# A two-layer graph-attention network: adjacency masks turned by the DMA engines instead of by TensorE

## The chip, the cores and the metric

The kernel runs on one core of one Trainium2 chip. The metric is the device time of one execution in microseconds; the kernel before took 3589.72 us (median of three runs, 3589.04 to 3592.5). PE is the matrix engine, PEld its weight loads, DVE the vector engine, ACT the scalar engine, POOL GpSimd, and SP the engine whose queue issues most DMA transfers.

## The reference, cut to what matters

N = 4096 nodes with 256 features. `adj` is a 4096 x 4096 matrix of zeros and ones in int32, the same for all attention layers. Three attention layers use it: one in network layer 0, two in network layer 1.

```python
x = x + _L0_gnn_ref(_layernorm(x), adj, ...)      # attention 1
x = x + _L0_ffn_ref(_layernorm(x), ...)           # 30 steps of tanh, silu, layernorm, 256x256 matmul
x = x + _L1_gnn_ref(_layernorm(x), adj, ...)      # attention 2 and 3
x = x + _L1_ffn_ref(_layernorm(x), ...)           # 6 experts, top 2
# one attention layer, 4 heads of 64 columns:
h = einsum('nf,hfd->hnd', x, W)
e = leaky_relu(f1[:, :, None] + f2[:, None, :], 0.2)
e = where(adj > 0, e, -9e15)
out = elu(einsum('hnm,hmd->hnd', softmax(e, axis=-1), h))
```

## The kernel before

**An attention layer.** The exponential of a leaky ReLU is one of two products, each with one factor for the row n and one for the column m. Which one holds depends on whether f1[n] + f2[m] is positive. So the kernel never builds e: for each pair it needs a 0/1 mask "edge and positive" and a 0/1 mask "edge and not positive", multiplies each with values already scaled by their column's factor (`vals`, in two fp16 parts), and combines the two sums at the end with the row's factor `r`.

**Tiling.** Columns m lie on the partitions in 32 blocks of 128, taken in pairs q = 0 to 15. Rows n are taken in chunks. A chunk's mask of the edges is held in SBUF as four tiles `m` of 8 blocks x chunk rows in bf16, columns on partitions, rows along the free dimension: that is `adj` turned. The main loop (line 522) runs over chunk, head and q. In one step ACT makes `st`, the step function of f1 + f2, two instructions (L464); DVE makes `m1` from `st` and `m` (L533) and `m2 = m - m1` (L538); PE multiplies each 128 x 128 block of m1 and m2, as weights, with `vals` and adds into PSUM (L565). For 6 of the 16 q the mask is kept negative (0 and -1, `turned(q)`, the sign is in `vals`): then m1 comes from a `logical_and`, m2 is not needed, and PE uses m itself. At the end of a head ACT and DVE take the sums out of PSUM (`lo` L474, `u` L475), DVE and ACT finish the rows (L482 to L495) and SP stores them.

**Where the masks come from.** In the first layer `adj` must be turned. `load_rows` (L203) fetches 256 columns of a chunk's rows with a casting DMA from POOL's queue, int32 to bf16. `turn` (L212) turns each 128 x 128 block on PE into PSUM (`tp_m`, L217). `to_mask` (L222) compares on DVE and writes the mask to SBUF. It is stored turned in DRAM, `edges[block, partition, row]` (L74). The first chunk's masks are made in the preparation of the layer (`first_masks`, L229, called at L423) and are used straight from SBUF. Those of chunk c + 1 are made inside the main loop on chunk c: `make` (L500) is a generator that advances one piece per step (L540), turning, comparing and storing block by block (L514). `load_mask` (L195) fetches four tiles of a chunk with plain copies; it is issued in the last head of the chunk before, each time one of the four buffers has been used for the last time (L573). The second and third layers only load. The first layer has chunks of 4, 7, 7, 7 and 7 row tiles (L607), the others four chunks of 8 (L766).

**Preparation.** Before each main loop, eight groups of 512 rows are normalised, turned and multiplied with the weights (L268 to L394). In the first layer, the masks of the first chunk are made in between.

**Order.** SP issues its transfers in program order, each waiting for its own data; so a store of masks, a mask load and a load of `f1b` (L193) follow each other there. Casting loads are issued by POOL.

Of the kernel before, what the change touches and what calls it, by code (L numbers as in the profile page):

```python
# [11 lines left out]
F32 = mybir.dt.float32  # L12
BF16 = mybir.dt.bfloat16
# [14 lines left out]
G = 4  # L28
# [16 lines left out]
def gnn_ffn_kernel(ctx: ExitStack, tc: tile.TileContext, a: dict, out: bass.AP):  # L45
    nc = tc.nc
    x, adj = a["x"], a["adj"]
    N = x.shape[0]
    NT = N // P
# [8 lines left out]

    ident = const.tile([P, P], F32, name="ident")
    make_identity(nc, ident)  # L60
    ident16 = const.tile([P, P], BF16, name="ident16")
    nc.gpsimd.tensor_copy(ident16, ident)
    mone = const.tile([P, 1], F32, name="mone")
    nc.gpsimd.memset(mone, -1.0)
    ones = const.tile([2 * H, P], F32, name="ones")
# [5 lines left out]

    edges = dram.tile([NT, P, N], BF16, name="edges")  # L74
    fd = dram.tile([2 * H, N], F32, name="fd")

    x1d = dram.tile([N, C], F32, name="x1d")
# [4 lines left out]
    def rows_of(t, g):  # L82
        return t[g * GR : (g + 1) * GR, :].rearrange("(r p) c -> p r c", p=P)
# [3 lines left out]
    def rows_in():  # L87
        return stream.tile([P, G * C], F32, name="rows")
# [33 lines left out]


    def turned(q):
        return q % 8 in (1, 4, 6)


    sign = const.tile([P, NT], F32, name="sign")
# [42 lines left out]
    def attention(tag, src, norm, w, others, chunks, first, finish, following):  # L171
# [6 lines left out]
        with ExitStack() as scope:  # L178
# [6 lines left out]
            fpool = scope.enter_context(tc.tile_pool(name=f"{tag}_f", bufs=2))  # L185

            end = None if first else scope.enter_context(tc.tile_pool(name=f"{tag}_end", bufs=1))
            masks, arow, f1b = {}, {}, {}

            def load_f1(c, h):  # L190
                n0, w = starts[c] * P, chunks[c] * P
# [3 lines left out]
            def load_mask(c, g):  # L195

                n0, w = starts[c] * P, chunks[c] * P
                m = masks[c, g] = mask.tile([P, 8, CM * P], BF16, name="m")
                nc.sync.dma_start(
                    m[:, :, :w], edges[g * 8 : (g + 1) * 8, :, n0 : n0 + w].rearrange("j p n -> p j n")  # L200
                )

            def load_rows(c, j):  # L203
                nt = chunks[c]
                arow[c, j] = rows_in().bitcast(BF16).rearrange("p (t n) -> p t n", n=2 * P)

                nc.gpsimd.dma_start(  # L207
                    arow[c, j][:, :nt, :],
                    adj[starts[c] * P : (starts[c] + nt) * P, j * P : (j + 2) * P].rearrange("(t p) n -> p t n", p=P),
                )  # L210

            def turn(pool, c, j):  # L212

                nt = chunks[c]
                tp = pool.tile([P, 8 * P], BF16, name="tp_m")
                for t in range(nt):
                    nc.tensor.transpose(  # L217
                        tp[:, t * P : (t + 1) * P], arow[c, j - j % 2][:, t, (j % 2) * P : (j % 2 + 1) * P], ident16
                    )
                return tp  # L220

            def to_mask(dst, tp, c, j):  # L222
                w = chunks[c] * P
                if turned(j // 2):
                    nc.vector.tensor_scalar(dst[:, :w], tp[:, :w], 0.0, -1.0, op0=OP.is_le, op1=OP.add)
                else:
                    nc.vector.tensor_scalar(dst[:, :w], tp[:, :w], 0.0, None, op0=OP.is_gt)

            def first_masks(pool, j):  # L229

                g = j // 8
                if j % 8 == 0:
                    masks[0, g] = mask.tile([P, 8, CM * P], BF16, name="m")
                for jj in (j, j + 1):
                    to_mask(masks[0, g][:, jj % 8, :], turn(pool, 0, jj), 0, jj)
                if j % 8 == 6:
                    w = chunks[0] * P
                    nc.sync.dma_start(
                        edges[g * 8 : (g + 1) * 8, :, :w].rearrange("j p n -> p j n"), masks[0, g][:, :, :w]
                    )  # L240

            with ExitStack() as ps:
                prep = ps.enter_context(tc.tile_pool(name=f"{tag}_prep", bufs=1))
# [4 lines left out]
                ps_m = ps.enter_context(tc.tile_pool(name=f"{tag}_ppm", bufs=1, space=PSUM))  # L248
# [9 lines left out]
                def load(g):  # L258
                    if g in ahead:
                        rows[g] = ahead.pop(g)  # L260
                    elif first:
                        rows[g] = work.tile([P, G, C], F32, name="t", bufs=3)
                        nc.sync.dma_start(rows[g], rows_of(src, g))
                    else:
                        load_ahead(src, g)
                        rows[g] = ahead.pop(g)
# [126 lines left out]
                            op1=OP.add,  # L393
                        )  # L394

                if first:
                    for j in range(0, 6, 2):
                        load_rows(0, j)
                load(0)
                load(1)  # L400
                if not first:
                    load_mask(0, 0)
                made_masks = 0
                late = [functools.partial(make, prep, small_ps, get(prep)) for get, make in others]
                if late:
                    late.pop(0)()
                for g in range(NG + 2):
                    if g + 2 < NG:
                        load(g + 2)
                    if 2 <= g < NG:  # L410
                        columns(g)
                    if 1 <= g <= NG:
                        now = products(g - 1)
                    if 2 <= g:
                        lower(g - 2)
                    if g < 2:
                        columns(g)
                    if 1 <= g <= NG:
                        upper(g - 1, *now)
                    if first:  # L420
                        for _ in range(2 if g in (1, 2, 3, 4, 5, 6) else 1):
                            if made_masks < NT:
                                first_masks(ps_m, made_masks)  # L423
                                if made_masks + 6 < NT:
                                    load_rows(0, made_masks + 6)
                                made_masks += 2
# [4 lines left out]
                if first:  # L431
                    assert made_masks == NT
# [15 lines left out]

            if first:
                end = scope.enter_context(tc.tile_pool(name=f"{tag}_end", bufs=1))  # L450
                made = scope.enter_context(tc.tile_pool(name=f"{tag}_made", bufs=2))
            work = scope.enter_context(tc.tile_pool(name=f"{tag}_work", bufs=2))
            ps_o = scope.enter_context(tc.tile_pool(name=f"{tag}_pso", bufs=1, space=PSUM))
            ps_m = scope.enter_context(tc.tile_pool(name=f"{tag}_psm", bufs=1, space=PSUM)) if first else None
# [44 lines left out]

            def make(c):  # L500

                n0, w = starts[c] * P, chunks[c] * P
                load_rows(c, 0)
                load_rows(c, 2)
                for j in range(NT):
                    if j % 2 == 0:
                        st = made.tile([P, 2, CM * P], BF16, name="ms")
                        if j + 4 < NT:
                            load_rows(c, j + 4)
                    tp = turn(ps_m, c, j)  # L510
                    yield
                    to_mask(st[:, j % 2, :], tp, c, j)
                    if j % 2 == 1:
                        nc.sync.dma_start(  # L514
                            edges[j - 1 : j + 1, :, n0 : n0 + w].rearrange("j p n -> p j n"), st[:, :, :w]
                        )
                    if j < NT - 4:
                        yield

            step_of(*units[0])  # L520
            closing, making = None, None
# [81 lines left out]
    for n in range(2):  # L603
        av = a[f"L1_gnn_a{n + 1}"]
        for got, to in zip(weights(f"g{n + 1}", a[f"L1_gnn_W{n + 1}"], av[:, :D], av[:, D:], not n), (gw, makers)):
            to.append(got)
    attention("g0", x, True, w0, [make, *makers], [4, 7, 7, 7, 7], True, to_rows(x1d, x), [x1d])  # L607

# [583 lines left out]
```

## Time and profile before

| part of the trace | time |
|---|---|
| preparation of attention 1, up to the first product with a mask (L565) | 126.4 us |
| main loop of attention 1 (20 heads) | 126.4 us to about 812 us |
| feed-forward scan | to about 1895 us |
| attention 2, main loop | about 1982 us to 2579 us |
| attention 3, main loop | about 2642 us to 3242 us |
| experts | to 3587.7 us |

| engine | busy | share of the span |
|---|---|---|
| PE | 3264.7 us | 91% |
| DVE | 3002.9 us | 84% |
| ACT | 2615.2 us | 73% |
| POOL | 1100.6 us | 31% |

The page lists groups of instructions as "line, engine, operation, output<-inputs, shapes, count | busy time, mean time of one | idle time of the engine before them, and who ended it". A table by stretches gives, for each stretch of time, its length and then the busy time of each engine with the number of its instructions, the granted PE clock as a share of full speed, the share of the DMA engines' time that was busy, and GB/s. A DMA view names each queue with its packets, its MB, and the share of the 16 DMA engines' time that its packets took; q1 is the hardware queue behind SP, q0 the software queue behind POOL.

### The profile page before, as it was taken

To read this page: it belongs to the slowest core of one execution; us is meant where nothing else is said; L and a number is where in the kernel's file an instruction comes from. 1 tells how busy PE (TensorE), PEld (TensorE's weight loads), DVE (VectorE), ACT (ScalarE), POOL (GpSimd) and SP (SyncE) were. 2 spreads that over 40 slices of the span, in tenths; PEclk is the share of its full clock that TensorE was granted. 3 is DMA by queue.
4 is the path that set the end of the run, shared out by engine and by line. 5 is a ranking of instruction groups with operands and counts; after the bars stand their busy time and mean duration, and the time that the engine had idled before them with its cause. 6 is when DMAs were issued, how large, how long until landed. Compare 5 with 4: busy or idle time off the path is not lost. (4 is left out here: it accounts for less than half of the span.)

```text
span 3587.7 us, 81089 instructions
## 1 busy us (share of the span) xinstructions
PE 3264.7 (91%) x33523; PEld 2981.2 (83%) x33523; DVE 3002.9 (84%) x6039; ACT 2615.2 (73%) x2902; POOL 1100.6 (31%) x899
## 2 busy tenths in 40 slices
PE   6889999996999999999998899999979999996895
PEld 5779889885888888888886889888878888884784
DVE  6899999997877777877786899999889999997445
ACT  2688888886766666666663999999789999993221
POOL 3211101005877777777761000000000000001662
PEclk8899999998999999999998999999999999997897
DMA  6897887501000000000015031321212231314224
GB/s 136 145 232 141 192 196 135 168 22 55 1 1 1 1 1 1 1 1 1 1 31 194 17 119 33 125 75 66 85 66 78 89 123 44 119 25 135 83 95 182
DMA packets 280202, 288.48 MB, mean 80 GB/s; under 512 B 97149, under 2 KB 230426, under 8 KB 279834
## 3 DMA queue, kind: packets, MB, share of 16 engines
q1 hardware_dynamic: 198770, 224.18, 19.2%
q0 software_dynamic: 73920, 52.97, 9.7%
q10 hardware_dynamic: 7144, 6.16, 0.6%
q8 instruction: 264, 4.33, 0.5%
q14 instruction: 104, 0.85, 0.1%
HBM read 248.01 MB, written 68.81 MB: 88 GB/s over the span
## 5 line engine op out<-in xcount | busy, mean ns | idle before, releaser
L565 PE MATMUL acc<-vals,m 128*128 128x130 f16 (+1 forms) x24576 | 1726.6, 232 | 128.2 <-DVE u L475 89.0
L565 PEld LDWEIGHTS <-m 128*128 128x128 bf16 x24576 | 1625.2, 98 | 215.6 <-issue 95.5
L464 ACT ACTIVATE st<-f1b,f2b 128x1024 bf16<-128x1024 f32 (+2 forms) x1664 | 1660.2, 1071 | 152.6 <-DVE m L533 144.8
L533 DVE TENSOR_TENSOR m<-st,m 128x2048 bf16<-128x2048 bf16 (+2 forms) x832 | 938.1, 1137 | 37.0 <-PE acc L565 28.4
L708 PE MATMUL po<-wT,zT 128*128 128x256 f32 x3840 | 875.1, 381 | 10.3 <-ACT zT L734 10.1
L708 PEld LDWEIGHTS po<-wT,zT 128*128 128x128 f32 x3840 | 715.8, 192 | 99.8 <-ACT zT L734 12.4
L694 POOL TENSOR_TENSOR th<-th,y 128x1024 f32<-128x1024 f32 x240 | 567.8, 2367 | 196.2 <-ACT th L693 195.4
L538 DVE TENSOR_TENSOR m<-m,m 128x2048 bf16<-128x2048 bf16 (+2 forms) x520 | 592.8, 1140 | 25.1 <-PE tp_m L217 0.5
L105 POOL TENSOR_TENSOR ln_rstd<-ln_rstd,mhalf 128x4 f32<-128x4 f32 x272 | 281.7, 1036 | 904.1 <-DVE ln_rstd L104 877.3
L100 DVE BATCH_NORM_STATS2 ln_st<-z 128x6 f32<-128x256 f32 x960 | 337.9, 413 | 191.3 <-ACT z L699 191.3
L734 ACT COPY zT<-tp 128x1024 f32<-128x1024 f32 x240 | 242.8, 1012 | 323.7 <-PE tp L113 323.7
L718 DVE SCALAR_TENSOR_TENSOR y<-po,ln_rstd,bias 128x256 f32<-128x256 f32 x928 | 378.6, 469 | 5.2 <-PE po L708 4.4
L699 ACT ACTIVATE z<-th 128x1024 f32<-128x1024 f32 x240 | 254.5, 1060 | 18.5 <-POOL th L694 18.2
L113 PE MATMUL tp<-ident,z 128*128 128x128 f32 x1920 | 251.2, 274 | 12.3 <-ACT z L699 12.3
L113 PEld LDWEIGHTS tp<-ident,z 128*128 128x128 f32 x1920 | 225.9, 142 | 38.9 <-ACT z L699 15.3
L693 ACT ACTIVATE th<-y 128x1024 f32<-128x1024 f32 x240 | 251.2, 1047 | 4.8 <-DVE y L718 4.7
L207 POOL DMA_DIRECT2D rows<-in_adj_dram x80 | 72.9, 912 | 490.6 <-PE tp_m L217 490.3
L447 POOL MEMSET hs<- 128x4 f32 x3 | 0.3, 101 | 630.5 <-DVE u L488 609.1
L305 PE MATMUL ph<-g_w,xT 128*128 128x264 f32 x384 | 112.6, 454 | 30.9 <-DVE v L375 27.7
L305 PEld LDWEIGHTS ph<-g_w,xT 128*128 128x128 f32 x384 | 84.5, 227 | 50.8 <-issue 16.6
L1076 ACT COPY w<-ew 128x512 f32 x37 | 22.7, 617 | 132.8 <-PE ph L1083 103.5
L475 DVE TENSOR_TENSOR u<-acc,lo 128x520 f32<-128x520 f32 (+1 forms) x104 | 66.6, 654 | 49.0 <-ACT lo L474 48.8
(209 smaller groups left out, 2141.6 us busy)
## 6 DMA issues: line engine op xcount, KB each, us to landing
m<-edges SPq DMA_DIRECT2D x32, 2048.0 KB
rows<-in_adj_dram POOLq DMA_DIRECT2D x64, 448.0 KB, 8.0
edges<-ms SPq DMA_DIRECT2D x64, 448.0 KB
m<-edges SPq DMA_DIRECT2D x16, 1792.0 KB
f1b<-fd SPq DMA_DIRECT2D x32, 512.0 KB
rows<-x1d SPq DMA_DIRECT2D x16, 512.0 KB
y<-yd SPq DMA_DIRECT2D x16, 512.0 KB
f1b<-fd SPq DMA_DIRECT2D x16, 448.0 KB
```

The source lines that it names most:

```text
L100: nc.vector.bn_stats(st[:, r, :], src[:, r, :])
L105: nc.gpsimd.tensor_tensor(rstd, rstd, mhalf, OP.pow)
L113: nc.tensor.transpose(ps[:, k, r * P : (r + 1) * P], src[:, r, k * P : (k + 1) * P], ident)
L464: nc.scalar.activation(st[:, s, :w], f1b[c, h][:, :w], AF.Relu, bias=f2b[:, 2 * q + s, h : h + 1], scale=BIG)
L533: nc.vector.tensor_tensor(m1[:, :, :w], st[:, :, :w], m, OP.logical_and if turned(q) else OP.min)
L538: nc.vector.tensor_tensor(m2[:, :, :w], m, m1[:, :, :w], OP.subtract)
L565: nc.tensor.matmul(acc[:, i, cols], lhs[:, s, rows], v[:, cols], start=(j == 0 and n_ == 0), stop=(j == NT - 1 and n_ == 1), skip_group_ch ...
L693: nc.scalar.activation(th[at], y[:, g * G : (g + 1) * G, :], AF.Tanh, scale=0.01)
L694: nc.gpsimd.tensor_tensor(th[at], th[at], y[:, g * G : (g + 1) * G, :], OP.add)
L699: nc.scalar.activation(z, th.pop(at - 1), AF.Silu, scale=0.01)
L708: nc.tensor.matmul(po[:, r, :], src[:, k, r * P : (r + 1) * P], wT[:, k, :], start=(k == 0), stop=(k == KC - 1),)
L718: nc.vector.scalar_tensor_tensor(y[:, g * G + r, :], po[:, r, :], rstd[:, r : r + 1], last if end else bias, op0=OP.mult, op1=OP.add,)
```

## The change

The masks are no longer turned before they are kept. They are kept in DRAM row by row, as `adj` itself lies (`edges` is N x N), and each load of a mask tile is a transposing DMA. PE's turning and its PSUM tiles go away, and with them the comparison of a PSUM tile; DVE compares in place in SBUF, on the rows as they were loaded. A load of rows takes 2048 columns of one row tile (half its width) instead of 256 columns of a whole chunk. `to_masks` compares in three instructions: the q that are not turned in one or two patterns, the turned ones in another; so that a pattern with a fixed step can pick them, `turned(q)` becomes `q % 3 == 0`, again 6 of 16. The first chunk's four row tiles are loaded whole into the buffers that later hold the masks, compared, stored and loaded back turned; they too go through DRAM now. With the PSUM tiles gone, the first layer's chunks can be of 8 row tiles: 4, 4, 8, 8, 8. The maker of the next chunk's masks handles a half row tile in every third step. The rows of `x` in the first layer now come through the shared `rows` buffers.

```diff
-    edges = dram.tile([NT, P, N], BF16, name="edges")
+    edges = dram.tile([N, N], BF16, name="edges")
...
     def turned(q):
-        return q % 8 in (1, 4, 6)
+        return q % 3 == 0
...
                 m = masks[c, g] = mask.tile([P, 8, CM * P], BF16, name="m")
+                nc.sync.dma_start_transpose(m[:, :, :w], edges[n0 : n0 + w, g * 8 * P : (g + 1) * 8 * P])
+
+            def load_edges(dst, t, q):
+                nq = dst.shape[1]
+                nc.gpsimd.dma_start(
+                    dst, adj[t * P : (t + 1) * P, q * 2 * P : (q + nq) * 2 * P].rearrange("p (q n) -> p q n", n=2 * P)
+                )
+
+            def to_masks(rows, t, q):
+                nq = rows.shape[1]
+                a = -q % 3
+                b = a + (nq - a) // 3 * 3
+                plain = [rows[:, a:b].rearrange("p (i r) n -> p i r n", r=3)[:, :, 1:]]
+                plain += [x for x in (rows[:, :a], rows[:, b + 1 :]) if x.shape[1]]
+                for x in plain:
+                    nc.vector.tensor_scalar(x, x, 0.0, None, op0=OP.is_gt)
+                x = rows[:, a::3]
+                nc.vector.tensor_scalar(x, x, 0.0, -1.0, op0=OP.is_le, op1=OP.add)
                 nc.sync.dma_start(
-                    m[:, :, :w], edges[g * 8 : (g + 1) * 8, :, n0 : n0 + w].rearrange("j p n -> p j n")
+                    edges[t * P : (t + 1) * P, q * 2 * P : (q + nq) * 2 * P].rearrange("p (q n) -> p q n", n=2 * P), rows
                 )
-            def load_rows(c, j):
-            def turn(pool, c, j):
-            def to_mask(dst, tp, c, j):
-            def first_masks(pool, j):
...
+                if first:
+                    staged = []
+                    for t in range(chunks[0]):
+                        if t % 2 == 0:
+                            m = mask.tile([P, 8, CM * P], BF16, name="m")
+                            m = m.rearrange("p j n -> p (j n)")[:, : 2 * N].rearrange("p (t n) -> p t n", t=2)
+                        staged.append(m[:, t % 2].rearrange("p (q n) -> p q n", n=2 * P))
+                        load_edges(staged[t], t, 0)
...
+                        if 2 <= g < 2 + chunks[0]:
+                            to_masks(staged[g - 2], g - 2, 0)
+                        if g == 2 + chunks[0]:
+                            for i in range(4):
+                                load_mask(0, i)
...
             def make(c):
-                n0, w = starts[c] * P, chunks[c] * P
-                load_rows(c, 0)
-                load_rows(c, 2)
-                for j in range(NT):
...
+                halves = [(starts[c] + t, q) for t in range(chunks[c]) for q in (0, NJ // 2)]
+                got = {}
+                for i in range(-2, len(halves)):
+                    if i + 2 < len(halves):
+                        t = rows_in().bitcast(BF16).rearrange("p (q n) -> p q n", n=2 * P)
+                        got[i + 2] = t
+                        load_edges(t, *halves[i + 2])
+                    if i >= 0:
+                        for _ in range(3):
+                            yield
+                        to_masks(got.pop(i), *halves[i])
...
-    attention("g0", x, True, w0, [make, *makers], [4, 7, 7, 7, 7], True, to_rows(x1d, x), [x1d])
+    attention("g0", x, True, w0, [make, *makers], [4, 4, 8, 8, 8], True, to_rows(x1d, x), [x1d])
```

More of the change, by code (lines that the diff above doesn't have):

```diff
@@ L60, in gnn_ffn_kernel @@
     make_identity(nc, ident)
-    ident16 = const.tile([P, P], BF16, name="ident16")
-    nc.gpsimd.tensor_copy(ident16, ident)
     mone = const.tile([P, 1], F32, name="mone")
@@ L187, in attention @@
             end = None if first else scope.enter_context(tc.tile_pool(name=f"{tag}_end", bufs=1))
-            masks, arow, f1b = {}, {}, {}
+            masks, f1b = {}, {}
             def load_f1(c, h):
@@ L199, in load_mask @@
                 nc.sync.dma_start(
-                    m[:, :, :w], edges[g * 8 : (g + 1) * 8, :, n0 : n0 + w].rearrange("j p n -> p j n")
+                    edges[t * P : (t + 1) * P, q * 2 * P : (q + nq) * 2 * P].rearrange("p (q n) -> p q n", n=2 * P), rows
                 )
-            def load_rows(c, j):
[L204 to L210, printed above, removed]
@@ L212, in turn @@
-            def turn(pool, c, j):
[L214 to L220, printed above, removed]
-            def to_mask(dst, tp, c, j):
[L223 to L227, printed above, removed]
@@ L229, in first_masks @@
-            def first_masks(pool, j):
[L231 to L240, printed above, removed]
@@ L247, in attention @@
                 ps_h = ps.enter_context(tc.tile_pool(name=f"{tag}_pph", bufs=1, space=PSUM))
-                ps_m = ps.enter_context(tc.tile_pool(name=f"{tag}_ppm", bufs=1, space=PSUM))
                 xs = prep.tile([P, KC, NG], F32, name="xs")
@@ L260, in load @@
                         rows[g] = ahead.pop(g)
-                    elif first:
-                        rows[g] = work.tile([P, G, C], F32, name="t", bufs=3)
-                        nc.sync.dma_start(rows[g], rows_of(src, g))
                     else:
@@ L394, in lower @@
                         )
-                if first:
-                    for j in range(0, 6, 2):
-                        load_rows(0, j)
                 load(0)
                 load(1)
-                if not first:
+                if first:
[6 more added lines that the diff above has]
+                        load_edges(staged[t], t, 0)
+                else:
                     load_mask(0, 0)
-                made_masks = 0
                 late = [functools.partial(make, prep, small_ps, get(prep)) for get, make in others]
@@ L420, in attention @@
                     if first:
[L421 to L426, printed above, removed]
+                        if 2 <= g < 2 + chunks[0]:
[3 more added lines that the diff above has]
+                                load_mask(0, i)
                     elif g in (2, 4, 6):
@@ L430, in attention @@
                         late.pop(0)()
-                if first:
-                    assert made_masks == NT
                 nc.vector.tensor_tensor(r, fs[:, :, :H], mb.to_broadcast([P, NT, H]), OP.add)
@@ L450, in attention @@
                 end = scope.enter_context(tc.tile_pool(name=f"{tag}_end", bufs=1))
-                made = scope.enter_context(tc.tile_pool(name=f"{tag}_made", bufs=2))
             work = scope.enter_context(tc.tile_pool(name=f"{tag}_work", bufs=2))
             ps_o = scope.enter_context(tc.tile_pool(name=f"{tag}_pso", bufs=1, space=PSUM))
-            ps_m = scope.enter_context(tc.tile_pool(name=f"{tag}_psm", bufs=1, space=PSUM)) if first else None
             units = [(c, h, q) for c in range(len(chunks)) for h in range(H) for q in range(NJ)]
@@ L500, in make @@
             def make(c):
-                n0, w = starts[c] * P, chunks[c] * P
-                load_rows(c, 0)
-                load_rows(c, 2)
-                for j in range(NT):
[L506 to L518, printed above, removed]
+                halves = [(starts[c] + t, q) for t in range(chunks[c]) for q in (0, NJ // 2)]
[9 more added lines that the diff above has]
+                        to_masks(got.pop(i), *halves[i])
             step_of(*units[0])
```

## The prediction, made before the result

> **What bounds the kernel now.** I read the page's 40 slices first, to see which stage the change can reach. A slice is 89.7 us. Slices 1 to 9 are the first attention layer, 10 to 21 the feed-forward scan, 22 to 36 the other two attention layers, the rest the experts.
>
> ```profile
> PE   6889999996999999999998899999979999996895
> DVE  6899999997877777877786899999889999997445
> ACT  2688888886766666666663999999789999993221
> DMA  6897887501000000000015031321212231314224
> ```
>
> In all three attention layers PE, DVE and ACT are full together. What sets the first layer apart is DMA: 50 to 100% busy there, a tenth to a third in the other two. The edit acts on the first layer, and on the mask loads of all three.
>
> Second, busy time in stretches of one head each. The timeline of the SP queue gives their lengths: the loads of `old` and `f1b` come 24.0 to 24.2 us apart in the 4-tile chunk, 37.35 in 7-tile chunks that also make masks, 34.7 in the last 7-tile chunk, which makes none, and 37.26 to 37.5 in the 8-tile chunks of the later layers.
>
> ```profile
> core 0: us, PE busy (x) PEld busy (x) DVE busy (x) ACT busy (x) POOL busy (x), PEclk, DMA share, GB/s
> 300.00:337.35 37.35, 35.17 (x508) 33.75 (x506) 35.44 (x44) 31.96 (x35) 3.72 (x4) 0.95 0.67 125
> 686.00:720.70 34.70, 31.70 (x445) 30.19 (x443) 31.66 (x36) 31.73 (x36) 0.00 (x0) 0.95 0.11 28
> 2200.00:2237.30 37.30, 35.10 (x517) 33.37 (x515) 35.14 (x36) 35.36 (x36) 0.00 (x0) 1.00 0.08 26
> 160.00:184.00 24.00, 21.32 (x312) 19.60 (x311) 22.86 (x44) 20.97 (x35) 3.72 (x4) 1.00 1.03 177
> ```
>
> Read down the DVE and PE columns: mask making adds 3.8 us of DVE and 3.5 us of PE to a 7-tile head, yet the head grows by only 2.65. Third, the chain of waits inside one 8-tile head, where no masks are made:
>
> ```profile
> 2195.92 10.50 ACT st L464 x10
> 2206.41 0.50 ACT lo L474
> ...
> 2206.93 0.71 DVE u L475
> ...
> 2207.69 17.63 PE acc L565 x256
> ...
> 2225.67 1.23 DVE m L533
> ```
>
> The head is a ring of three nearly equal engines. At the head's end it narrows to lo, u, then the next matmul; there DVE waits 1.25 us for ACT and PE 1.8 us for DVE. Slack per engine is about 2 us, so work beyond that on one engine lengthens the head.
>
> **What the Trainium skill says.** "VectorE: DVE Perf Modes", section "The perf-mode tier table": a `tensor_scalar` on bf16 runs 4 elements a cycle from SBUF, at most 2 when an operand is in PSUM. The trace shows the PSUM half (896 columns in 618 ns, below) and no bf16 `tensor_scalar` in SBUF. "DMA: Bandwidth & Descriptors", section "Latency and other measured facts": a DMA transpose was measured at 261 GB/s with a non-contiguous middle dimension, 350 to 400 contiguous. The trace has no DMA transpose.
>
> **The change, part by part.** Removed from the first layer:
>
> ```profile
> L217 PE MATMUL tp_m<-ident,rows 128*128 128x128 bf16 x1024 | 86.1, 223 | 20.8 <-DVE ms L225 8.7 <-DVE ms L227 7.0 <-DVE m L227 3.0
> L227 DVE TENSOR_SCALAR ms<-tp_m 128x896 bf16<-128x896 bf16 x80 | 49.4, 618 | 2.4 <-PE tp_m L217 2.2
> L225 DVE TENSOR_SCALAR ms<-tp_m 128x896 bf16<-128x896 bf16 x48 | 29.7, 619 | 10.0 <-DMA edges<-ms 6.4 <-PE tp_m L217 2.9 <-PE acc L565 0.6
> ```
>
> *Compares.* Added: three in-place compares per half row tile, of 1024, 256 and 768 columns. At 4 a cycle of 0.96 GHz that is 0.267, 0.067 and 0.2 us, plus a start-to-start cost that I take from the 2048-column `tensor_tensor` (1.135 us apart in DVE's timeline, 1.067 of it streaming), rounded up for the wait between them to 0.095. Sum 0.82 us a half; at 2 a cycle 1.35. An 8-tile chunk has 16 halves: 13.1 us, 3.3 a head. The eight evictions that go cost 3.8 a head by the two rows above.
>
> *Heads of 8 tiles with masks (chunks 2 and 3).* DVE 35.1 + 3.3, the 1.25 wait for lo, some 0.4 of hand-overs: 40.0 us, DVE-bound; PE (512 slots, 35.1) gains from the lost transposes but cannot use it. Eight heads: 320. *The last chunk*, without masks: 37.3, at this layer's clock of 0.95 instead of 1.00 some 38: 152. *Heads of 4 tiles:* DVE 22.9 - 3.8 = 19.1, plus 1.65 when the next chunk has 4 tiles, 3.3 when it has 8; ACT stays at 21.0. With 1.3 us of boundary that is ACT-bound 22.3, then DVE-bound 23.7: 89 + 95. *First rows of a chunk:* a compare stands in DVE's order, so m and u of the following steps queue behind it, and PE behind those. A row load of 448 KB took 8.0 us to land; the first compare comes three steps (4 to 7 us) after its load: about 4 us at each of three chunks, 12. Sum 668. Before, from the first L565 at 126.4 us to the last head's end at about 812: 686. **Loop: -18.**
>
> *Preparation.* fd is written every 12.3 us on average here (30.9 to 117 us for eight groups), every 9.4 in the second layer, which makes no masks. With four row tiles to compare at 1.4 us each, I take 10.5: seven gaps, -13. The first chunk's rows are now 8 MB of adj asked for in the first microseconds, beside the weights for which ACT already waits 18.6 us: +1 to +10, taken as +3. The first masks must go adj, SBUF, compare, DRAM, turned load; the fifth iteration ends near 75 us, the four 1 MB loads can land by 100, the loop starts near 115: hidden. **Preparation: -10.**
>
> *Row transfers.* The same 64 MB of adj, in runs of 8 KB in place of 1 KB, on POOL's queue at 0.9 us an issue: hidden, except perhaps in the second 4-tile chunk. It fetches 16 MB in 93 us beside stores of 8 MB. At the old rate (the software queue's 9.7% of the span for all of adj, 348 us) that is 87 + 20 us, 14 too many; with long runs I expect it to fit.
>
> *Turned loads.* Nine chunk switches each load four groups of 2 MB for an 8-tile chunk. A load is issued when its buffer comes free, every fourth step, 9.3 us apart; group g is needed 12 steps, 28 us, after the first issue plus 9.3 g. With L us per load the last lands at 4 L and is needed at 56: no stall up to L = 14. The price from both sides:
>
> ```profile
> q1 hardware_dynamic: 1184, 0.79, 7.4%
> ...
> q1 hardware_dynamic: 2224, 1.05, 10.8%
> ...
> q1 hardware_dynamic: 5344, 9.18, 63.2%
> ```
>
> These are the DMA views of a 37.26 us head in the second layer, a 37.5 us head in the third, which adds 1024 reads of 256 bytes, and a 42 us stretch with four plain mask loads. Plain: about 6 us each. A 256-byte read: (10.8% x 37.5 - 7.4% x 37.26) x 16 / 1040 = 20 ns; a 256-byte write, from the first line less f1b, some 23. If the turn reads its 2 MB as 8192 pieces of 256 bytes, L = 8192 x 20 / 16 = 10.3 us; if reads and writes add up, 22. The skill's 261 GB/s gives 8.0. I take 8 to 10: no stall. *Which q are turned* changes too, but 6 of 16 as before: nothing, within 0.3 us a head (+-10).
>
> Forecast: 3590 - 18 - 10 = **3562 us**.
>
> **Rivals.**
> 1. *The turned loads are too slow (slower than before).* At L = 16: 8 us of stall x 9 switches = 72, so 3630. At L = 22: 32 x 9, with some 20 in the 4-tile switch, so about 3870; PE would stand still at each chunk's first head, waiting for m. For it: no such DMA in the trace, and the first layer's DMA is up to 94% busy in a head. Against: the threshold is 50% above the slow single-pass price.
> 2. *DVE takes back what PE gives (no change).* Compares at 2 a cycle add 0.53 us x 48 halves = 25, or rows land late by that much: about 3587.
> 3. *More gain.* DVE's idle at the boundary absorbs part of the compares (38.7 a head, -10) and preparation runs at the second layer's 9.4 us (-8): 3544.
>
> **How the numbers follow.** Forecast 0.52, slow loads 0.13 at L near 16 and 0.13 near 22, no change 0.15, more gain 0.07. The forecast's own unknowns (compare price, start, row landing) are worth about +-25. The range runs from 3525 to 3700: it leaves out the slowest loads and little else. Faster by over 0.2% (7 us): the forecast nearly whole, more gain, a quarter of no change, 0.59. Within: half of no change and a little of the forecast, 0.08. Slower: 0.33.
>
> **What would show it.** Right: 8-tile heads of the first layer at about 40 us with DVE the fullest and PE idle more; later heads still 37.3 to 37.5; no wait of DVE for a DMA into m; compares at about 0.42, 0.22 and 0.36 us. Wrong: DVE m <- DMA m<-edges among the longest waits, a gap at each chunk switch, mask loads over 14 us; or compares near 1.2 us for 1024 columns; or a first L565 later than 126 us.

## The result, and the profile after

The kernel became slower: 3680.93 us against 3589.38 us, a ratio of 1.026 (95% interval 1.0238 to 1.0283). The forecast was 3562 us. The time lies inside the range, but on the other side of the kernel before.

The 40 slices of the changed kernel's page, for the same four rows as in the prediction:

```profile
PE   5578689987999999999997899999979989986895
DVE  5688689987877777787786899898889989987545
ACT  2488588986766666666653999999778999994221
DMA  8899871501000000000017051524241542604224
```

PE is less busy than before in slices 1 to 6 and 9, and has eights in slices 33 and 36, in the third layer, where it had nines. DMA is at least 80% busy in the first five slices. Stage by stage, in us, from the first and last products with a mask in the PE timeline of each trace:

| kernel | first product at | loop 1 | from there to layer 2's first product | loop 2 | preparation 3 | loop 3 |
|---|---|---|---|---|---|---|
| before | 126.4 | 685.0 | 1170.6 | 596.7 | 63.1 | 600.6 |
| after | 148.0 | 705.9 | 1180.1 | 615.2 | 64.5 | 622.7 |
| difference | +21.6 | +20.9 | +9.5 | +18.5 | +1.4 | +22.1 |

These sum to 94 us; the experts' stage gives a few back. So the loss is spread over the stages, and 40 us of it lie in the loops of layers 2 and 3, where the arithmetic is the same as before. There, the chain of waits of the changed kernel (start us, us, what) through a head's end:

```profile
2254.51 11.53 ACT st L438 x11
2266.04 0.49 ACT lo L448
...
2266.56 0.71 DVE u L449
...
2267.31 17.55 PE acc L533 x256
...
2304.08 0.49 ACT lo L448
```

In the kernel before, the `lo` after the one at 2206.41 us in the prediction's chain stands here:

```profile
2243.68 0.50 ACT lo L474
```

From one `lo` to the next are 38.04 us now; before, they were 37.27. Other heads of this loop take up to 39.4, so that the loop loses 18.5 us over its 16 heads. The last run of `st` in the chain has 11 members where it had 10. No DMA stands in the chain. The groups of the same kernel, with shapes kept apart, give the new compares and the wait for `lo`:

```profile
L213 DVE TENSOR_SCALAR rows<-rows 128x1024 bf16<-128x1024 bf16 x56 | 23.6, 422 | 57.9 <-DMA rows<-in_adj_dram 55.2 <-PE ph L279 2.7
L215 DVE TENSOR_SCALAR rows<-rows 128x768 bf16<-128x768 bf16 x56 | 23.3, 417 | 0.0
L213 DVE TENSOR_SCALAR rows<-rows 128x256 bf16<-128x256 bf16 x56 | 12.3, 219 | 0.0
...
L449 DVE TENSOR_TENSOR u<-acc,lo 128x520 f32<-128x520 f32 x88 | 61.1, 696 | 98.3 <-ACT lo L448 98.3
```

A compare costs what was forecast; ahead of the compares DVE stood still 55.2 us for rows of `adj`, and ahead of `u` it waited 98.3 us for `lo` (48.8 before). The SP queue at a chunk switch of layer 2 (start us, us, operation):

```profile
2162.66 7.76 SPq L197 DMA_TRANSPOSE m<-edges  x1
...
2171.15 17.48 SPq L197 DMA_TRANSPOSE m<-edges  x2
2188.74 0.52 SPq L191 DMA_DIRECT2D f1b<-fd  x1
2189.35 11.25 SPq L197 DMA_TRANSPOSE m<-edges  x1
```

and the DMA view of a 51 us window around it:

```profile
q1 hardware_dynamic: 34080, 9.18, 90.7%
```

The four turned loads move 8.4 MB in 256-byte pieces; the rate in that window reaches 290 GB/s while they run, about 7.2 us for 2 MB. Before, a plain load of the same tile held SP for 0.37 us. A turned one holds it 7.8 to 11.3 us here, and what is queued behind it waits: `f1b` is issued at 2188.74, right after a turned load.

### The profile page after: what moved, and what is told of

It reads as the page before. It is cut to its first block, busy times and chain, and to the rows that moved or that the text cites. A ratio compares the mean times of both kernels' runs of the same rounds, so it can differ in the third digit from the quotient of the medians.

```text
span 3677.5 us, 79140 instructions
## 1 busy us (share of the span) xinstructions
PE 3236.4 (88%) x32499; PEld 2938.7 (80%) x32499; DVE 2962.9 (81%) x6055; ACT 2617.4 (71%) x2902; POOL 1058.4 (29%) x878
## 5 line engine op out<-in xcount | busy, mean ns | idle before, releaser
L438 ACT ACTIVATE st<-f1b,f2b 128x1024 bf16<-128x1024 f32 (+1 forms) x1664 | 1662.5, 1071 | 216.2 <-DVE m L501 208.0
L501 DVE TENSOR_TENSOR m<-st,m 128x2048 bf16<-128x2048 bf16 (+1 forms) x832 | 932.7, 1134 | 62.7 <-PE acc L533 33.0
L676 PEld LDWEIGHTS po<-wT,zT 128*128 128x128 f32 x3840 | 715.6, 191 | 104.3 <-ACT zT L702 14.3
L506 DVE TENSOR_TENSOR m<-m,m 128x2048 bf16<-128x2048 bf16 (+1 forms) x520 | 592.0, 1138 | 24.4 <-PE acc L533 0.5
L449 DVE TENSOR_TENSOR u<-acc,lo 128x520 f32<-128x520 f32 (+1 forms) x104 | 67.7, 653 | 98.3 <-ACT lo L448 98.3
L202 POOL DMA_DIRECT2D rows<-in_adj_dram x56 | 30.6, 546 | 330.4 <-DVE m L506 74.7
```

The costliest lines, as they stand in the source:

```text
L438: nc.scalar.activation(st[:, s, :w], f1b[c, h][:, :w], AF.Relu, bias=f2b[:, 2 * q + s, h : h + 1], scale=BIG)
L501: nc.vector.tensor_tensor(m1[:, :, :w], st[:, :, :w], m, OP.logical_and if turned(q) else OP.min)
L506: nc.vector.tensor_tensor(m2[:, :, :w], m, m1[:, :, :w], OP.subtract)
L676: nc.tensor.matmul(po[:, r, :], src[:, k, r * P : (r + 1) * P], wT[:, k, :], start=(k == 0), stop=(k == KC - 1),)
```

## The experiments

There are five candidates: the order of the turned q, the time at which compares run, the first loads, the jump in chunk size, and SP held by turned loads. Each ratio below is to the kernel before, measured again beside the runs of that experiment. It took 3586 to 3594 us from one time to another, so differences in us between experiments are good to some 5.

### The order alone, in the kernel before

```diff
 # kernel before
-        return q % 8 in (1, 4, 6)
+        return q % 3 == 0
```

> The kernel before with one line changed: turned(q) is q % 3 == 0. If the order of the turned steps is what lengthens the heads (the second layer's went from 37.26 to 38.04 us, the third's from 37.5 to 38.3 and 39.7), this kernel shows the same heads with plain loads and no turned DMA at all, and gets slower by 35 to 60 us: 3625 to 3650. If the longer heads come from the turned loads (DMA traffic, or SP held while it issues them), the heads stay at 37.26 and 37.5 and the time within 5 us of 3590.

Measured: 3645.72 us, ratio 1.0148 (1.0131 to 1.0165). No compare, no turned load and no chunk was changed, and 51 us are gone: loop 2 is 615.4 and loop 3 625.2, close to the changed kernel's. Loop 1 lost only 3.6 us (688.6). What the prediction costed at nothing is the largest single loss.

### The order put back, in the changed kernel

```diff
-        return q % 3 == 0
+        return q % 8 in (1, 4, 6)
 # to_masks: the same compares on these q, in five patterns per eight q
```

> The changed kernel with the old order of turned steps, q % 8 in (1, 4, 6); a half row tile is then compared in five instructions instead of three (1.06 us of DVE by the measured 0.42 and 0.22 us, against 0.82). Order theory: heads of the second layer back to 37.3, of the third to 37.5, total down by 35 to 55 us, to 3625 to 3645. Rival (turned loads or the start alone): heads stay at 38.0 and 39.7, total 3681 to 3690 because of the two extra instructions.

Measured: 3620.3 us, ratio 1.0074 (1.0057 to 1.009), some 61 us less than the changed kernel (65 when each is set against its own measurement of the kernel before), with two compares more in each half. Loops 2 and 3 are 596.9 and 600.6, those of the kernel before to 0.2 us, with all their turned loads. So the turned loads cost these loops nothing, and loop 1 falls to 686.4. The loss of 26 us that is left lies in the start of the first layer (15.3 us in the trace), in the second preparation (9.0) and in the third (3.1).

### The weights first

```diff
-                        load_edges(staged[t], t, 0)
...
+                    if first and g == 0:
+                        with tc.issue_after(pows[0]):
+                            for t in range(chunks[0]):
+                                load_edges(staged[t], t, 0)
```

> The changed kernel, but the four 2 MB loads of adj for the first chunk are queued on POOL behind the first rows' power (some 16 us in) instead of in the first 2 us. If the late start (first store of fd at 51.6 us instead of 30.9) comes from weights standing behind 8 MB of adj in the DMA engines, the first store of fd comes at 31 to 35 us and the total falls by 12 to 20 us, to 3661 to 3669. If it comes from the x rows now going through the shared buffers, the first store stays near 51 us and the total at 3681.

Measured: 3685.12 us, ratio 1.0262 (1.0236 to 1.0287): no gain. The first store of `fd` did come earlier (41.1 us instead of 51.6; 30.9 before), and the first product too (138.9 instead of 148.0), but loop 1 grew by the same 9 us (714.7) and ended at 853.5, as without the edit. Something in loop 1 set its end by itself. The store also missed the 31 to 35 us that were expected: the weights are half of its delay. ACT's wait for them, in the changed kernel and in this one, and what DVE waited for here:

```profile
ACT L250 <- DMA g_w<-in_L_gnn_W_dram: 33.7, 1, 33.7
...
ACT L250 <- DMA g_w<-in_L_gnn_W_dram: 14.6, 1, 14.6
...
DVE m L213 <- DMA m<-in_adj_dram: 9.8, 3, 4.3
```

(The kernel before waited 18.6 us for its weights.) The compares of the first row tiles now stood on DVE ahead of work that the store needs, and waited for rows still on their way.

### The compares held to their step

In the text one half row tile is compared every third step. In the trace, the second chunk's eight halves are compared at 98 to 142 us, before the first product, and the third chunk's sixteen at 146 to 237 us: about a chunk ahead of the text, since the instructions are put on their engines in an order that a scheduler makes. DVE of the changed kernel, in order of time (start us, us, instruction, and in brackets the idle time before it):

```profile
162.27 0.68 DVE L501 TENSOR_TENSOR m<-st,m 128x1024 bf16<-128x1024 bf16 x1
164.38 0.43 DVE L213 TENSOR_SCALAR rows<-rows 128x1024 bf16<-128x1024 bf16 x1 [1.43 <-DMA rows<-in_adj_dram]
164.73 0.68 DVE L506 TENSOR_TENSOR m<-m,m 128x1024 bf16<-128x1024 bf16 x1
...
177.49 0.43 DVE L213 TENSOR_SCALAR rows<-rows 128x1024 bf16<-128x1024 bf16 x1 [2.79 <-DMA rows<-in_adj_dram]
177.83 0.68 DVE L501 TENSOR_TENSOR m<-st,m 128x1024 bf16<-128x1024 bf16 x1
```

A compare whose rows have not landed holds up the m1 and m2 behind it, and PE behind those. The edit ties each piece, with its loads and stores, to its step:

```diff
-                nc.vector.tensor_tensor(
+                here = nc.vector.tensor_tensor(
                     m1[:, :, :w], st[:, :, :w], m, OP.logical_and if turned(q) else OP.min
-                )
+                ).ins
...
-                    next(making, None)
+                    with tc.issue_after(here):
+                        next(making, None)
```

> The changed kernel, but each half's compares are queued on DVE right behind the step that the program writes them in, so that they lie every third step of the chunk before, instead of up to a whole chunk earlier and in a row. Bunching theory (DVE stood 55 us before compares whose rows had not landed, and the first product waited 16.6 us for DVE): the waits of DVE for rows fall below 25 us, the first product comes 10 us sooner, heads of the third chunk fall from 56, 50 and 45 us to about 41, total down by 20 to 40 us, to 3641 to 3661. Rival (the compares only take time that someone has to give): heads with compares grow to 41 to 42 everywhere and the total stays within 10 us of 3681.

Measured: 3658.24 us, ratio 1.0181 (1.0164 to 1.0198), 23 us less than the changed kernel (28 by the ratios). The waits of DVE for rows and for masks, from 120 to 860 us, first in the changed kernel:

```profile
DVE rows L213 <- DMA rows<-in_adj_dram: 52.0, 20, 5.6
...
DVE m L501 <- DMA m<-edges: 8.2, 2, 4.5
```

then in this one (total us, times, longest):

```profile
DVE m L501 <- DMA m<-edges: 14.3, 1, 14.3
...
DVE rows L213 <- DMA rows<-in_adj_dram: 3.9, 3, 2.0
```

Nearly all of the wait for rows is gone; loop 1 is 677.8 us, and the first product comes at 135.4, so that loop 1 ends 40.7 us earlier than in the changed kernel. The whole gained less because loop 2, which the edit does not touch, took 623.5 us in this trace (624.1 in the trace above, 615.2 in the changed kernel); why is open. One wait has taken its place, once, for 14.3 us: the mask of the first 8-tile chunk. The SP queue of this kernel there:

```profile
298.71 24.51 SPq L197 DMA_TRANSPOSE m<-edges  x1
...
323.96 23.98 SPq L197 DMA_TRANSPOSE m<-edges  x3
```

One turned load held SP for 24.5 us, while rows of `adj` were being fetched.

### Order and pace together

The edits of the second and fourth experiment in one kernel.

> The two largest causes taken out together: the set of turned q as in the kernel before, and each compare queued behind the m1 of its step. If they are separate costs (order -61 us, pacing -23 us, each measured alone), about 3681 - 84 = 3597 us (3588 to 3606), first layer's loop about 655 us, heads with masks near 40 us, DVE waiting under 5 us for rows. Rival: both take out the same waits at the head's boundary, so that the second brings little: 3612 or more.

Measured: 3593.65 us, ratio 1.0009 (0.9992 to 1.0026). In the whole the two losses add up, to within 4 us of the 3597 expected. In loop 1 they do not: it takes 672.9 us where 655 were expected of this run, so there the two took out some of the same waits. (The prediction's own sum for this loop was 668.) The wait for the first 8-tile mask is still there (14.0 us, once).

### Mask loads later in the text of the preparation

```diff
-                else:
-                    load_mask(0, 0)
...
-                    elif g in (2, 4, 6):
-                        load_mask(0, g // 2)
+                    elif g == 6:
+                        load_mask(0, 0)
+                    elif g == 9:
+                        for i in range(1, 4):
+                            load_mask(0, i)
```

> As e7, and in the second and third layer's preparation the mask loads come after the row loads and most of the stores of fd on the SP queue. If it is SP, held by each turned load, that makes the second preparation 9 us longer than before (and the third some 3), then 9 to 12 us less than e7: about 3586, with the second layer's first product about 1171 us after the first layer's loop ends, as before. Rival: the preparation is longer for another reason (DMA engines shared with the turned loads): no change against e7. Third: the masks now come too late for the loop, with DVE waiting for m: slower than e7 by 10 or more.

Measured: 3588.77 us, ratio 0.999 (0.9977 to 1.0004), not told apart from the one above; the second layer's first product comes 1176.6 us after loop 1 (1177.5 there). The edit did not do what it was for. The SP queue of this kernel:

```profile
1886.78 8.75 SPq L197 DMA_TRANSPOSE m<-edges  x1
1895.58 0.56 SPq L698 DMA_DIRECT2D x2d<-rows  x1
...
1899.62 10.81 SPq L197 DMA_TRANSPOSE m<-edges  x1
...
1911.64 8.82 SPq L197 DMA_TRANSPOSE m<-edges  x1
```

The loads moved in the text, but SP still took three of them up among the stores of `x2d` and the loads of rows. So the order in which SP takes up its transfers is not that of the kernel's text, as the description of the kernel before had it. The run settles nothing about SP; a later one holds the loads back by force.

### A second chunk of another size

```diff
-... [4, 4, 8, 8, 8], True, ...
+... [4, 6, 7, 7, 8], True, ...
```

> As e8, with the first layer in chunks of 4, 6, 7, 7, 8 tiles in place of 4, 4, 8, 8, 8. If the jump from a 4-tile chunk to an 8-tile chunk (16 MB of adj, 8 MB of stores and 8 MB of turned loads within some 93 us) makes the stall at the second switch, the wait of DVE for m there (14 us) goes and the loop is 8 to 15 us shorter than e8's. Rival: the smaller chunks have more heads' ends worth nothing and the load is the same in sum: within 3 us of e8.

Measured: 3581.18 us, ratio 0.9974 (0.9967 to 0.9982), 8 us less than the run above; the two intervals just overlap, but in the traces loop 1 falls from 670.3 to 658.7, and no wait of DVE for `m<-edges` is left. A 4-tile chunk lasts some 93 us (four heads of 23.3 in the paced kernel's trace) and was to fetch 16 MB of `adj`, store 8 MB and load 8 MB turned for the 8-tile chunk after it.

### The weights first, again

The edit of the third experiment on top of the kernel above.

> As e9, and the first chunk's rows of adj are asked for only after the first group's statistics, so that the weights come first. With the compares paced and the larger second chunk, the loop no longer takes the gain back: first product 9 us earlier and the end 6 to 10 us earlier than e9. Rival: as without pacing, the loop takes it back: within 3 us of e9.

Measured: 3569.02 us, ratio 0.9938 (0.9918 to 0.9958). The first product comes at 120.6 us instead of 132.7, and loop 1 keeps the gain (660.7). The edit that was worth nothing in the changed kernel is worth 12 us here. That it is so because the compares no longer run into rows still under way is likely, not isolated: this kernel differs from the earlier one in order and chunk sizes too.

### The mask loads held back by force

```diff
+                        with tc.issue_after(stores[g - 1]):      # g = 5 to 8; the store of fd of group g - 1
+                            load_mask(0, g - NG + 3)
```

> As e10, and the mask loads of the second and third layer's preparation are queued only after the stores of fd of the fifth to eighth group (in e8 the program's order had changed but SP still took the loads up early, at 1886.8 us). If the turned loads, holding SP for 9 to 11 us each, are what makes the second preparation some 7 us longer than before and the third 3 us, the second layer's first product comes 1171 to 1173 us after the first layer's loop ends (1179 in e10), and the whole is 6 to 10 us less: about 3561. Rival: the DMA engines that the turned loads share with the row loads make it, or another cause: within 3 us of e10.

Measured: 3557.8 us, ratio 0.991 (0.9888 to 0.9932). SP of this kernel now alternates:

```profile
1911.78 7.65 SPq L197 DMA_TRANSPOSE m<-edges  x1
1920.01 0.62 SPq L323 DMA_DIRECT2D fd<-rt  x1
1920.68 7.48 SPq L197 DMA_TRANSPOSE m<-edges  x1
1928.25 0.59 SPq L323 DMA_DIRECT2D fd<-rt  x1
1928.89 7.84 SPq L197 DMA_TRANSPOSE m<-edges  x1
```

The second layer's first product comes 1168.4 us after loop 1, where the kernel above took 1179.4 and the kernel before 1170.6. So the 9.5 us came from turned loads taken up early in the preparation. On SP's queue they stood ahead of needed work: in the kernel above the last store of `x2d` was issued 1095.3 us after loop 1, right after a turned load, and in this one at 1087.6 (1087.8 before). But no wait for a DMA of that length shows on the engines (DVE waited 2.7 us for rows of `x2d` in the run with the loads moved in the text, 1.7 before), and holding the loads back also keeps them off the DMA engines while rows are fetched. Whether SP or the shared DMA engines did it is not separated. The third preparation gained nothing (67.6 against 66.2), against what was expected of it.

### Which step of a head is turned

```diff
 # kernel before, two runs
-        return q % 8 in (1, 4, 6)
+        return q % 8 in (1, 4, 7)      # the last step of a head turned, the first not
+        return q % 8 in (0, 3, 6)      # the first turned, the last not
```

> The kernel before with q = 1, 4, 7, 9, 12, 15 turned: the last step of a head is turned, the first of the next is not. If two turned steps in a row at the head's boundary are what cost 51 us in e1, this stays within 10 us of before (heads 37.3 to 37.5). If a turned last step alone does it (ACT is asked for the next st sooner, just when it has to make lo): 30 to 55 us slower, heads near 38.3.

> The kernel before with q = 0, 3, 6, 8, 11, 14 turned: the first step of a head is turned, the last of the one before is not. Two turned in a row as the cause: within 10 us of before. A turned first step alone as the cause (its products need m1 alone, and come before u has freed the accumulators): 30 to 55 us slower.

Measured: 3638.69 us, ratio 1.0143 (1.012 to 1.0165), and 3582.72 us, ratio 0.9984 (0.9971 to 0.9997). The two orders have the same gaps between turned steps, one being the other moved by one step, so what differs is their place against the head's end. With the last step turned and the first not, 47 us are lost; with the first turned and the last not, none, and loop 2 is 10 us shorter. That two turned steps meet, my own favourite, is not the cause. The 47 us are a balance: in its trace the first of the two kernels lost 29.7 and 30.7 us in loops 2 and 3 (626.4 and 631.3), but gained 12.1 in loop 1 (672.8). So a turned last step is not dear everywhere; why loop 1 gained was not looked into. The waits for `u` and for `m` from 2000 to 2500 us, some 13 heads (total us, times, longest), in the kernel before:

```profile
PE acc L565 <- DVE u L475: 22.0, 13, 1.9
...
ACT st L464 <- DVE m L533: 24.9, 52, 1.1
```

with the last step turned:

```profile
PE acc L565 <- DVE u L475: 43.2, 26, 3.1
...
ACT st L464 <- DVE m L533: 52.0, 52, 1.9
```

with the first step turned:

```profile
PE acc L565 <- DVE u L475: 26.5, 14, 3.0
...
ACT st L464 <- DVE m L533: 18.2, 40, 0.8
```

Both waits double with the last step turned. With the first step turned PE waits slightly longer than before for `u`, and ACT less for `m`.

### Both, as the fastest version

The order 0, 3, 6 in the kernel that holds the mask loads back; a half is then compared in three instructions instead of five.

> As e11, with q = 0, 3, 6, 8, 11, 14 turned in place of 1, 4, 6, 9, 12, 14: the last step of a head stays unturned, the first becomes turned. If what counts is the last step alone, the gain that the kernel before had from this order (second layer's loop -10 us, first layer's -7, third layer's none) comes again: some 10 to 17 us less than e11, about 3545. Rival: the heads of the new first layer are bound by DVE (masks) and the gain there is gone: 3548 to 3555. If a turned first step costs something in this kernel: above 3558.

Measured: 3551.03 us, ratio 0.9896 (0.9879 to 0.9912). It beats the kernel before by 1%. Whether the order adds anything to the run that holds the masks back (0.991) is not told apart: loop 2 gained its 10 us again (586.8), but in this trace loop 1 and the two preparations are each 2 to 4 us longer. The 3545 us that were expected were not reached.

## Why the prediction was wrong, step by step

**The step that failed.** "*Which q are turned* changes too, but 6 of 16 as before: nothing, within 0.3 us a head (+-10)." I counted operations and not where they stand. In the changed kernel a head lost 1.2 us on average in loop 2 and 1.4 in loop 3. A turned step needs one operation of DVE, another two (1.13 us more, start to start). With q = 15 turned, DVE comes to the head's end early and ACT late. The end of a head in the kernel before, in the timelines of the three engines:

```profile
2191.76 14.66 ACT L464 ACTIVATE st<-f1b,f2b 128x1024 bf16<-128x1024 f32 x14
...
2191.79 14.13 PE L565 MATMUL acc<-vals,m 128*128 128x130 f16 x207
...
2206.32 0.58 ACT L474 ACTIVATE lo<-acc 128x520 f32<-128x520 f32 x1
...
2206.93 0.70 DVE L475 TENSOR_TENSOR u<-acc,lo 128x520 f32<-128x520 f32 x1 [1.25 <-ACT lo L474]
...
2207.69 6.50 PE L565 MATMUL acc<-vals,m 128*128 128x130 f16 x93 [1.76 <-DVE u L475]
```

and in the changed kernel:

```profile
2251.39 14.65 ACT L438 ACTIVATE st<-f1b,f2b 128x1024 bf16<-128x1024 f32 x14
...
2251.79 12.73 PE L533 MATMUL acc<-vals,m 128*128 128x130 f16 x189
...
2265.95 0.58 ACT L448 ACTIVATE lo<-acc 128x520 f32<-128x520 f32 x1
...
2266.56 0.70 DVE L449 TENSOR_TENSOR u<-acc,lo 128x520 f32<-128x520 f32 x1 [2.20 <-ACT lo L448]
...
2267.31 6.92 PE L533 MATMUL acc<-vals,m 128*128 128x260 f16 x99 [2.79 <-DVE u L449]
```

PE's products ended at 2205.92 us before and `lo` began 0.40 us later; in the changed kernel they ended at 2264.52 and `lo` began 1.43 later, since ACT's run of `st` lasted 1.52 us beyond PE's products (0.50 before). DVE waited 2.20 us for it instead of 1.25, PE 2.79 for `u` instead of 1.76, and then ACT twice for DVE's `m1` (0.71 and 1.02 us), where before it waited once (0.80). The prediction had read this very spot as the ring's narrow place, and put "Slack per engine is about 2 us" beside it; it should have followed the new order through it. Runs show that the order costs it: 51 us alone in the kernel before, some 61 back in the changed kernel, and 47 for an order with the last step turned against none for the same order moved by one. That the extra `st` ahead of `lo` is the way it does so is read off the timelines, not taken apart further.

**First rows of a chunk, 12 us.** The mechanism, a compare that stands in DVE's order ahead of m and u, was right, its size wrong: DVE waited 55.2 us in 22 places, not 12 in three. The step assumed that compares run where the text has them, three steps after their load; they ran a chunk earlier, through rows still on their way. Tying them to their step takes off some 23 us alone and 27 with the order put back. So the second rival, that DVE takes back what PE gives, came true in the half that the prediction mentioned in passing: rows that land late.

**Start +3, preparation -10.** The first product came 21.6 us later, the prediction's own sign of being wrong ("later than 126 us"). The first store of `fd` was 20.7 us late, twice the upper end of "+1 to +10". About half of it was the weights, held up by the 8 MB asked for at once; with the weights first it was still 10.2 us late, with DVE standing 9.8 us at compares of rows that had not landed. The pace after it was right (10.9 us between stores, forecast 10.5). At its end came what was not in the sum, the second chunk's compares ahead of the first product; held to their steps, it came 12.6 us earlier. With the weights first too, and the other chunks, it came at 120.6, 5.8 before the old time.

**Turned loads, 8 to 10 us, no stall.** Right for the loops of layers 2 and 3: 7.2 us at 290 GB/s, 7.5 to 11.8 of SP; 90.7% of 51 us on 16 engines over 34080 pieces is 21.7 ns each, where I had worked out 20. The figure of 261 GB/s in the Trainium skill ("DMA: Bandwidth & Descriptors", "Latency and other measured facts") was a little low for this shape. The first rival, turned loads too slow, did not come about in the later layers; that the measured time lies inside the range is luck, for the range reached so far up on its account. In the first it did in part: DVE waited 8.2 us for `m<-edges` in the changed kernel, where one load held SP for 14.47 us. What the step left out is that SP issues nothing else meanwhile; turned loads taken up early in the second preparation cost 9.5 us. Beside casting loads, one took 24.5 us in the paced kernel; so the "second 4-tile chunk", where I had left it at "I expect it to fit", did not fit, for some 8 us.

**Compares, 0.82 us a half.** Right: in DVE's timeline from 160 to 180 us what follows them starts 0.35, 0.14 and 0.34 us after them (1024, 256 and 768 columns), 0.83 in sum. The 768 columns take as long as the 1024, where I had less for them. At the 4 elements a cycle that the Trainium skill ("VectorE: DVE Perf Modes", "The perf-mode tier table") gives for bf16 in SBUF, and the 0.96 GHz of its "Specifications", 1024 columns would stream in an estimated 0.27 us, at 2 a cycle in 0.53. The 0.35 measured leaves only the first, and this half of the second rival falls.

**The loop, 668 us.** With order and pace mended it took 672.9, 14.0 of them one wait for a mask, with heads of 39.7 to 41.1 us from `lo` to `lo` while masks are made and 37.5 in the last chunk, where 40.0 and 38 were worked out. In one such head of 40.2 us DVE was busy 39.8 and PE 36.0: DVE-bound, as forecast. So the part of the argument on the compares and on what sets the head stands; the changed kernel hid it behind the other losses. One after the other, the ratios to the kernel before went 1.026, 1.0074 (order), 1.0009 (pace), 0.9974 (chunk sizes, with the mask loads moved in the text), 0.9938 (weights first), 0.991 (masks held back).

**Two readings without consequence.** The ninth slice, which the prediction counts to the first layer, shows a DMA share of 0 and not "50 to 100%". The 3.8 us a head for the evictions that go is the difference of DVE's busy time between two stretches (35.44 and 31.66); "the two rows above" it give durations, and 8 x 0.618 would be 4.9.

## What to carry to other kernels

Where several engines turn in a ring with a microsecond or two of slack, an edit that keeps every count can still cost more than the one it comes with: follow the new order through the ring's narrow place before calling it free. A step in the text is not a place in time; if prefetched work must not run ahead of its data, tie it to an instruction of its step. And price a transfer twice, for its landing and for the queue that issues it, with what waits behind it there.

## What the runs showed of the hardware

Issuing a transposing DMA of 2 MB held the SP queue for 7.5 to 11.8 us in layers 2 and 3 of the changed kernel, where such transfers ran at up to 290 GB/s (7.2 us for 2 MB). One held it 24.5 us in the paced kernel, while casting loads shared the DMA engines. A plain load of the same tile held it 0.36 to 0.52 us in these layers of the kernel before.

A compare over three separate runs of 256 columns took 417 ns, as long as one over two runs of 512 (422 ns). The two are also different operations, so the runs are not shown to be the reason.

The clock granted to PE differed between stretches of the changed kernel: 0.55 of full speed from 126 to 150 us, where PE was busy 5.8 of 24.0 us, 0.86 from 310 to 480 us (busy 121.9 of 170.0), and 1.00 in a head of the second layer (busy 34.9 of 38.0). Which of the two follows from the other, and what it costs, was not measured.
